# Finer hand-over steps in a sixteen-image, four-layer pipeline on one core

## The chip, the core and the metric

The kernel runs on one core of a Trainium2 chip. The core has a matrix engine (PE, with its weight loads shown as PEld), a vector engine (DVE), a scalar engine (ACT), a general engine (POOL) and a queue engine (SP); sixteen DMA engines move data for SP, ACT and POOL. Each engine works through its own queue in order, and semaphores tie the queues together. The metric is the device time of one execution in microseconds (us). The kernel before took 5924.86 us (median of three runs, 5919.08 to 5937.79).

## The reference

The input is 16 images of 64 x 64 positions (4096 tokens) with 256 channels, all float32. Four layers follow each other, each of the form `x = x + layer(_gn(x))`, where `_gn` is a group norm with 32 groups over a whole image:

```python
# layer 0: nearest of 1024 codes, whose row is added
dis = sum(xf*xf) + sum(e*e, axis=0) - 2*matmul(xf, e);  out = e.T[argmin(dis)]
# layer 1: attention inside each row of 64 positions, sigmoid instead of softmax
attn = sigmoid((x@Wf+bf) @ (x@Wg+bg).T);  out = attn @ (x@Wh+bh)
# layer 2: one scalar gate per token
sm = softmax(x0[:, :, None] * x1[:, None, :], axis=1)
out = sigmoid(einsum('bn,bnm->bm', x2, sm)) * x
# layer 3: linear attention with 4 heads of 32, then a layer norm with scale and shift
q = softmax(q, over head channels)*SCALE;  k = softmax(k, over tokens)
out = layernorm((context(k, v) @ q) @ w_out + b_out) * gamma + beta
```

Because every layer norms over a whole image, no layer can begin on an image before the layer ahead has ended on it.

## The kernel before, in words

One image is cut into 8 chunks (`NCHUNK`) of 512 tokens, each of 4 tiles (`CH`) of 128 tokens. A chunk in channel-major form is a tile of 128 partitions x 2 halves (`k` = 0, 1) x 512 tokens. The work is written as Python generators, one for each stage of one image:

- `stats0` (L287) loads an image's chunks and takes the statistics for the first norm.
- `stage1` (L303) is the search. For each tile T, ACT writes `nn` (L372), PE multiplies the normed chunk `xn` with the codes into `pd` (L377, two banks of PSUM), DVE adds the two and finds the maximum (`nd`, L384), DVE finds its index (L389), and POOL starts a gather that adds the code's row into the token tile `xc` (L390). Once in each chunk there is more: `norm` makes `xn` (L322) and its square `sq` (L325) on ACT, PE sums the squares (`px`, L331), ACT copies the sums (`xrow`, L336) and PE transposes them (`pxt`, L338), from where DVE copies them in `norm_rows` (L343); `back` transposes the four token tiles of the chunk before (`pt`, L352), ACT copies them over the chunk (L355), DVE takes the next norm's statistics (`chunk_stats`, L249), and ACT starts the store (L358).
- `layer1` (L416): `attend` makes `fg` and `h` and the sigmoid `at`; `mix` (L498) multiplies (`po`, L506), adds on DVE (L511), takes statistics and loads the chunk after next.
- `rows2` (L540) makes the three rows of layer 2 for an image: `pr` (L565), `rows` on ACT (L569), three small stores, transposes `prt` (L574) and a DVE copy `x01` (L575).
- `stage2` (L592) is the exponentials: 64 pairs of one ACT exponential of 128 x 2048 (L617) and one DVE product sum (L620).
- `gate2` (L653): each chunk is loaded, `gb` (the gate, broadcast) is loaded, and for each half ACT makes `u` (L674) and DVE applies it (L675); then statistics and a store.
- `stage3` (L689) is layer 3. Its first loop makes `kx` (L746), `qv` (L759 to L764), transposes `kx` (L770, L772), takes the maximum of the queries (`qm`, L778, DVE), subtracts it on POOL (L779), takes the exponential on ACT (L780) and multiplies keys with values (`pc`, L784). `normalize` (L728, POOL) and `queries` (L716, L718) follow one chunk later. The second loop makes the output.

Each `yield n` in a generator says how much work the step before it stood for. A heap at the end of the kernel (L877 on) gives every stage of every image a start and a length, and takes the generators' steps in the order of these times; so several images are always in work, each in another stage, and a step between two yields stays together. The framework's scheduler then orders the instructions of each engine from that order, by priority and by when it takes operands and buffers to be there. The order in a queue is fixed when the kernel is built.

Buffers that matter here: the tag `t4` has 5 slots of 4 KB and is shared by `nn`, `nd`, `sq`, `fg` and `rows`; small PSUM tiles (`bank`) share 4 banks; `pd`, `ph` and layer 1's `po` (`wide`) share 2 slots of two banks; `xa` (search chunks) has 3 slots, `xc` 2, `gb` 1. A wait for a slot is a wait for the last reader of what was in it.

Of the kernel before, what the change touches and what calls it, by code (L numbers as in the profile page):

```python
# [16 lines left out]
P = 128  # L17
# [4 lines left out]
CH = 4  # L22
# [19 lines left out]
def kernel(  # L42
# [244 lines left out]
    def stats0(b):  # L287
# [3 lines left out]
        for ch in range(NCHUNK):  # L291
            xt = xb.tile([P, NK, CW], F32, tag="xb", name=f"xs_{tag}_{ch}")
            nc.sync.dma_start(out=xt, in_=src[:, :, ch * CW : (ch + 1) * CW])
            chunk_stats(st, xt, ch)
            yield 1.5
# [7 lines left out]
    def stage1(b):  # L303
# [4 lines left out]
        xt, xc, xn, nx2, pxt = {}, {}, {}, {}, {}  # L308
# [9 lines left out]
        def norm(ch):  # L318
            xn[ch] = s1p.tile([P, NK, CW], F32, tag="xn", name=f"xn_{tag}_{ch}")
            sq = s1p.tile([P, NK, CW], F32, tag="t4", name=f"sq_{tag}_{ch}", bufs=5)  # L320
            for k in range(NK):
                nc.scalar.activation(  # L322
                    xn[ch][:, k, :], xt[ch][:, k, :], AF.Identity, bias=nbias[:, k : k + 1], scale=scale[:, k : k + 1]
                )
                nc.scalar.activation(  # L325
                    sq[:, k, :], xt[ch][:, k, :], AF.Square, bias=nbias[:, k : k + 1], scale=scale[:, k : k + 1]
                )
            px = bank(f"px_{tag}_{ch}")
            for t in range(CH):
                for k in range(NK):  # L330
                    nc.tensor.matmul(  # L331
                        px[32 * t : 32 * t + 32, :P], lhsT=neg32, rhs=sq[:, k, t * P : (t + 1) * P],
                        start=(k == 0), stop=(k == NK - 1),
                    )
            xrow = small.tile([P, P], F32, tag="xrow", name=f"xrow_{tag}_{ch}", bufs=1)
            nc.scalar.copy(xrow, px[:, :P])  # L336
            pxt[ch] = bank(f"pxt_{tag}_{ch}")
            nc.tensor.transpose(pxt[ch][:, :P], xrow, ident)  # L338

        def norm_rows(ch):  # L340
            px = pxt.pop(ch)
# [6 lines left out]
        def back(ch):  # L348
            for k in range(NK):
                pt = bank(f"pt_{tag}_{ch}_{k}")  # L350
                for t in range(CH):
                    nc.tensor.transpose(  # L352
                        pt[:, t * P : (t + 1) * P], xc[ch][:, t, k * P : (k + 1) * P], ident
                    )
                nc.scalar.copy(xt[ch][:, k, :], pt)  # L355
            chunk_stats(st1, xt[ch], ch)
            d = dram.tile([P, NK, CW], F32, tag=f"x1_{ch}", name=f"x1_{tag}_{ch}")
            nc.scalar.dma_start(out=d, in_=xt.pop(ch))  # L358
            x1_d[b].append(d)
# [3 lines left out]
        norm(0)  # L363
# [3 lines left out]
        for ch in range(NCHUNK):  # L367
            for t in range(CH):
                T = ch * CH + t

# [25 lines left out]
                if t == 1 and ch > 0:  # L396
                    back(ch - 1)
                    yield 2
                if t == 2 and ch + 1 < NCHUNK:
                    norm(ch + 1)  # L400
                    yield 2
                if t == 3:
                    if ch + 1 < NCHUNK:
                        norm_rows(ch + 1)
                        tokens(ch + 1)
                    if ch + 2 < NCHUNK:
                        load(ch + 2)
        back(NCHUNK - 1)
# [7 lines left out]
    def layer1(b):  # L416
# [34 lines left out]
        def attend(ch):  # L451
# [10 lines left out]
            for n in range(2):  # L462
                part = slice(2 * n * CK, 2 * (n + 1) * CK)
                nc.scalar.activation(fg[:, n, :], pfg[part, :HW], AF.Identity, bias=bfg_n[part, :])
            ph = wide(f"ph_{tag}_{ch}").rearrange("p (t c) -> p t c", c=C)
# [12 lines left out]
            yield 5  # L478
# [19 lines left out]
        def mix(ch):  # L498
# [12 lines left out]
            nc.vector.tensor_tensor(X, po.rearrange("p r m i -> p m r i"), X, ALU.add)  # L511
            chunk_stats(st2, xt[ch], ch)
# [10 lines left out]
        for ch in range(NCHUNK):  # L523
# [6 lines left out]
            yield 3  # L530
# [9 lines left out]
    def rows2(b):  # L540
# [17 lines left out]
        for h in range(2):  # L558
# [11 lines left out]
            for n in range(3):  # L570
                nc.scalar.dma_start(out=rd[n, h], in_=rows[n : n + 97 : 32, :])
            pt = bank(f"prt_{tag}_{h}")
# [6 lines left out]
            yield 4  # L579
# [12 lines left out]
    def stage2(b, parts=1):  # L592
# [19 lines left out]
        for part in range(parts):  # L612
# [30 lines left out]
            if rest is not None and part >= parts // 2 - 1:  # L643
                yield next(rest)
# [300 lines left out]
```

## Time and profile before

| | |
|---|---|
| median of the runs | 5924.86 us |
| the profiled execution | 5928.44 us, of which the profile's span is 5926.7 us |
| PE busy | 5337.4 us, 90% of the span |
| DVE busy | 5121.1 us, 86% |
| ACT busy | 4570.8 us, 77% |
| POOL busy | 1939.4 us, 33% |
| mean granted clock of PE | 0.941 |
| moved by DMA | 1059.47 MB, mean 179 GB/s |

How to read it: an engine's busy time is the time in which it executes an instruction. The idle time before an instruction is put down to what released it (the "releaser"). A busy PE is not PE at its peak, since matmuls overlap. With four to six stages in work, idle time on an engine only costs something where that engine or one that waits for it sets the pace.

### The profile page before, as it was taken

The numbers are of one execution on the slowest core, as the hardware profiler recorded it, in microseconds if no ns is written. First come the engines' busy times: TensorE is split into PE (matmuls) and PEld (weight loads), VectorE is DVE, ScalarE is ACT, GpSimd is POOL, SyncE is SP. The second block draws the span as 40 slices with busy tenths as digits, with TensorE's granted clock in tenths as the row PEclk, the third lists the DMA queues.
The fourth block names the chain that finished last, engine by engine and source line by source line (L and its number), as shares of the span: only waits on it lengthen the run. The fifth ranks groups of instructions, "written<-read, shape, count | busy, mean of one in ns | idle before, by whom it ended". The sixth has DMA issues, their size and how long they took to land.

```text
span 5926.7 us, 79561 instructions
## 1 busy us (share of the span) xinstructions
PE 5337.4 (90%) x28239; PEld 3211.1 (54%) x28239; DVE 5121.1 (86%) x7282; ACT 4570.8 (77%) x6754; POOL 1939.4 (33%) x1314
## 2 busy tenths in 40 slices
PE   8968899889999999998989999898999989997777
PEld 3524465545656565564656556565555646564555
DVE  6499798989989898898989889898998989888882
ACT  4377687878778787887879788797878878787873
POOL 3122233224233332433334233342424333231331
PEclk9989999989999898999999899999999999998899
DMA  6544745555656656565665656656565664644543
GB/s 186 162 124 124 225 137 177 184 184 162 207 168 192 197 151 202 184 207 181 184 205 167 194 183 188 206 174 204 164 210 164 202 204 147 209 158 173 184 158 116
DMA packets 521380, 1059.47 MB, mean 179 GB/s; under 512 B 52504, under 2 KB 266392, under 8 KB 512792
## 3 DMA queue, kind: packets, MB, share of 16 engines
q1 hardware_dynamic: 406288, 885.11, 44.7%
q0 software_dynamic: 73728, 67.14, 7.9%
q10 hardware_dynamic: 40968, 102.13, 4.5%
q8 instruction: 224, 3.67, 0.3%
q14 instruction: 172, 1.41, 0.1%
HBM read 751.18 MB, written 303.04 MB: 178 GB/s over the span
## 4 chain that ended last, share of the span: by engine, by line
PE 48%; DVE 16%; ACT 12%; DMA 7%; issue 6%; POOL 4%; ACTq 0%; SPq 0%; POOLq 0%; DVEq 0%
PE pd_s L377 15%; DVE ex_s L620 6%; ACT ex_s L617 5%; PE ph_l L468 5%; PE pqv_s L759 3%; PE po_s L854 3%; PE pk_s L737 3%; PE po_l L506 2%; PE pr_r L565 2%; DMA xr_r<-x_l 2%; DVE i_s L389 2%; POOL qv_s L779 2%; PE pvr_s L834 1%; PE pz_s L826 1%; DMA qo_s<-qd_s 1%
## 5 line engine op out<-in xcount | busy, mean ns | idle before, releaser
L620 DVE CUSTOM_DVE_ANT_0 ex_s<-ex_s,x2b 128x2048 f32<-128x2048 f32 x1024 | 2350.7, 2302 | 46.2 <-ACT ex_s L617 44.9
L617 ACT ACTIVATE ex_s<-x0b,nmax_s,x_r 128x2048 f32<-128x2048 f32 x1024 | 2137.8, 2088 | 66.4 <-DVE num_s L620 60.3
L377 PE MATMUL pd_s<-e,xn_s 128*128 128x512 f32 x4096 | 2022.2, 623 | 43.5 <-DVE m L384 40.8
L390 POOL DMA_INDIRECT xc_s<-in_emb_rows,i_s x512 | 1058.1, 2067 | 2063.9 <-DVE i_s L389 1466.8
L377 PEld LDWEIGHTS pd_s<-e,xn_s 128*128 128x128 f32 x4096 | 754.4, 197 | 764.9 <-issue 669.1
L384 DVE CUSTOM_DVE_ANT_0 nd_s<-pd_s,nn_s 128x1024 f32<-128x1024 f32 x512 | 622.2, 1215 | 174.4 <-ACT nn_s L372 82.1
L389 DVE FIND_INDEX8 i_s<-m,nd_s 128x8 uint32<-128x1024 f32 x512 | 624.1, 1219 | 0.0
L372 ACT ACTIVATE nn_s<-ne,nx_s 128x1024 f32<-128x1024 f32 x512 | 583.2, 1141 | 21.5 <-DVE nx_s L343 15.7
L468 PE MATMUL ph_l<-wh_l,xt_l 128*128 128x256 f32 x2048 | 525.5, 393 | 28.3 <-DVE m L384 16.5
L759 PE MATMUL pqv_s<-wqv_s,xk_s 128*128 128x256 f32 x2048 | 494.6, 382 | 0.0
L759 PEld LDWEIGHTS pqv_s<-wqv_s,xk_s 128*128 128x128 f32 x2048 | 390.9, 192 | 127.5 <-issue 65.5
L468 PEld LDWEIGHTS ph_l<-wh_l,xt_l 128*128 128x128 f32 x2048 | 380.9, 193 | 143.8 <-issue 57.5
L837 POOL TENSOR_TENSOR lrs_s<-lrs_s,mhalf 128x4 f32<-128x4 f32 x128 | 183.0, 1429 | 749.3 <-ACT lrs_s L836 710.5
L857 ACT ACTIVATE y_s<-po_s,lrs_s 128x256 f32<-128x256 f32 x512 | 237.1, 469 | 214.8 <-PE po_s L854 166.2
L854 PE MATMUL po_s<-wctx_s,qo_s 128*128 128x256 f32 x1024 | 336.0, 415 | 32.3 <-ACT y_s L857 31.1
L506 PE MATMUL po_l<-at_l,h_l 64*128 64x64 f32 x4096 | 318.5, 297 | 46.2 <-DVE xt_l L511 42.7
L506 PEld LDWEIGHTS po_l<-at_l,h_l 64*128 64x128 f32 x4096 | 286.5, 206 | 108.5 <-DVE xt_l L511 48.9
L779 POOL TENSOR_TENSOR qv_s<-qv_s,qm_s 128x512 f32<-128x512 f32 x128 | 232.7, 1818 | 312.3 <-DVE qm_s L778 181.7
L728 POOL TENSOR_TENSOR qv_s<-qv_s,qd_s 128x512 f32<-128x512 f32 x128 | 199.8, 1561 | 304.6 <-DVE qd_s L727 252.9
L865 DVE TENSOR_TENSOR y_s<-pxo_s,y_s 128x512 f32<-128x512 f32 x256 | 175.2, 686 | 125.0 <-ACT y_s L857 123.2
L854 PEld LDWEIGHTS po_s<-wctx_s,qo_s 128*128 128x128 f32 x1024 | 178.2, 198 | 172.5 <-ACT y_s L857 84.7
L737 PE MATMUL pk_s<-xk_s,wk_s 128*128 128x512 f32 x512 | 269.6, 650 | 0.0
(195 smaller groups left out, 7519.8 us busy)
## 6 DMA issues: line engine op xcount, KB each, us to landing
xs_s<-in_xT SPq DMA_DIRECT2D x128, 512.0 KB
xt_s<-in_xT SPq DMA_DIRECT2D x128, 512.0 KB
xc_s<-in_x SPq DMA_DIRECT2D x128, 512.0 KB
x_s<-xt_s ACTq DMA_DIRECT2D x128, 512.0 KB
xt_l<-x_s SPq DMA_DIRECT2D x128, 512.0 KB
x_l<-xt_l SPq DMA_DIRECT2D x128, 512.0 KB
xr_r<-x_l SPq DMA_DIRECT2D x128, 512.0 KB
xg_g<-x_l SPq DMA_DIRECT2D x128, 512.0 KB
```

What stands on the lines that cost most here:

```text
L372: nc.scalar.activation(nn, ne2, AF.Identity, bias=nx2[ch][:, t : t + 1])
L377: nc.tensor.matmul(pd[:, cols], lhsT=xn[ch][:, k, t * P : (t + 1) * P], rhs=e2[:, k, cols], start=(k == 0), stop=(k == NK - 1),)
L384: nc.vector.tensor_tensor_reduce(out=nd, in0=pd, in1=nn, scale=1.0, scalar=-3.0e38, op0=ALU.add, op1=ALU.max, accum_out=m8[:, 0:1],)
L389: nc.vector.max_index(i8, m8, nd)
L390: nc.gpsimd.indirect_dma_start(out=xc[ch][:, t, :], out_offset=None, in_=emb_rows, in_offset=bass.IndirectOffsetOnAxis(ap=i8[:, 0:1], axis=0),
L468: nc.tensor.matmul(ph[:, t, :], lhsT=X[:, k, t * P : (t + 1) * P], rhs=wh_n[:, k, :], start=(t % 2 == 0 and k == 0), stop=False, skip_grou ...
L506: nc.tensor.matmul(po[:, r, k * CH + t, :], lhsT=h[rows, t, k * P : (k + 1) * P], rhs=at[rows, t, :], start=True, stop=True,)
L617: nc.scalar.activation(ex, x0b, AF.Exp, bias=nmax[:, T : T + 1], scale=x01[:, T, 1:2], accum_out=den[:, h, T : T + 1])
L620: nc.vector.tensor_tensor_reduce(out=ex, in0=ex, in1=x2b, scale=1.0, scalar=0.0, op0=ALU.mult, op1=ALU.add, accum_out=num[:, h, T : T + 1],)
L737: nc.tensor.matmul(pk, lhsT=wk_n[:, k, :], rhs=xt[:, k, :], start=(k == 0), stop=(k == NK - 1))
L759: nc.tensor.matmul(pqv[:, j, :], lhsT=xt[:, k, t * P : (t + 1) * P], rhs=wqv_n[:, k, :], start=(j == 0 and k == 0), stop=False, skip_group ...
L854: nc.tensor.matmul(po[:, j, :], lhsT=qT[:, t * P : (t + 1) * P], rhs=wctx[:, 1, :], start=True, stop=True)
```

## The change

No arithmetic is changed. Every engine issues the same number of instructions as before (17117 on PE, 6772 on DVE, 6005 on ACT, 1351 on POOL and 1827 on SP in the built programs, before PE's instructions are split in two); what changes is where steps end, in which step an instruction lies, and a few buffers.

- `stats0` and `gate2` yield after each half of a chunk. In `gate2` the second half's `u` is written over `gb`, which gets 2 slots; `u` gets 1.
- In `stage1`, `norm` is done in halves, after tiles 1 and 2 of the chunk before; the sums of the squares (`norm_sums`) come ahead of tile 3; the transposition of the sums moves to `norm_rows` after tile 3. `back` does two tiles at a time, both halves in one bank, after tiles 0 and 1; its statistics come after tile 2. `load` of the chunk after next comes ahead of tile 3, and `tokens` after tile 2, both one tile earlier than before.
- `layer1` yields between `fg` and `ph`, and between `mix` and its statistics and load. `rows2` yields ahead of its transposes. `stage2` of the last image takes twice as many steps of `gate2`, which are half as long.
- `stage3` yields between `kx` and `qv`, between the two halves of `qv`, and after the maximum; `queries` comes after the subtraction, and the exponential after `pc`.

```diff
@@ stats0
-            chunk_stats(st, xt, ch)
-            yield 1.5
+            for k in range(NK):
+                nc.vector.bn_stats(st[:, k, ch, :], xt[:, k, :])
+                yield 0.75
@@ stage1
-        def norm(ch):
-            for k in range(NK):
+        def norm(ch, k):
+            if k == 0:
...
+            for out_, func in ((xn[ch], AF.Identity), (sq[ch], AF.Square)):
                 nc.scalar.activation(
...
+        def norm_sums(ch):
...
-            pxt[ch] = bank(f"pxt_{tag}_{ch}")
-            nc.tensor.transpose(pxt[ch][:, :P], xrow, ident)
...
         def norm_rows(ch):
-            px = pxt.pop(ch)
+            px = bank(f"pxt_{tag}_{ch}")
+            nc.tensor.transpose(px[:, :P], xrow.pop(ch), ident)
...
-        def back(ch):
+        def back(ch, pr):
+            pt = bank(f"pt_{tag}_{ch}_{pr}").rearrange("p (k n) -> p k n", k=NK)
             for k in range(NK):
-                pt = bank(f"pt_{tag}_{ch}_{k}")
-                for t in range(CH):
+                for j in range(2):
                     nc.tensor.transpose(
-                        pt[:, t * P : (t + 1) * P], xc[ch][:, t, k * P : (k + 1) * P], ident
+                        pt[:, k, j * P : (j + 1) * P], xc[ch][:, 2 * pr + j, k * P : (k + 1) * P], ident
                     )
-                nc.scalar.copy(xt[ch][:, k, :], pt)
-            chunk_stats(st1, xt[ch], ch)
+            nc.scalar.copy(xt[ch][:, :, 2 * pr * P : 2 * (pr + 1) * P], pt)
+            if pr == 1:
...
+                if t == 3:
+                    if ch + 2 < NCHUNK:
+                        load(ch + 2)
+                    if more:
+                        norm_sums(ch + 1)
+                        yield 0.7
...
                 yield 4
-                if t == 1 and ch > 0:
-                    back(ch - 1)
-                    yield 2
-                if t == 2 and ch + 1 < NCHUNK:
-                    norm(ch + 1)
-                    yield 2
-                if t == 3:
-                    if ch + 1 < NCHUNK:
-                        norm_rows(ch + 1)
+                if t < 2 and ch > 0:
+                    back(ch - 1, t)
+                    yield 0.7
+                if t in (1, 2) and more:
+                    norm(ch + 1, t - 1)
+                    yield 0.7
+                if t == 2:
+                    if more:
                         tokens(ch + 1)
-                    if ch + 2 < NCHUNK:
-                        load(ch + 2)
+                    if ch > 0:
+                        chunk_stats(st1, xt.pop(ch - 1), ch - 1)
+                        yield 0.7
+                if t == 3 and more:
+                    norm_rows(ch + 1)
@@ layer1
+            yield 1.5
             ph = wide(f"ph_{tag}_{ch}").rearrange("p (t c) -> p t c", c=C)
...
-            yield 5
+            yield 3.5
...
+
+        def after(ch):
             chunk_stats(st2, xt[ch], ch)
             if ch + 2 < NCHUNK:
                 load(ch + 2)
...
             mix(ch)
-            yield 3
+            yield 1.5
+            after(ch)
+            yield 1.5
@@ rows2
+            yield 2
             pt = bank(f"prt_{tag}_{h}")
...
-            yield 4
+            yield 2
@@ gate2
-            gb = s3p.tile([P, CW], F32, tag="gb", name=f"gb_{tag}_{ch}", bufs=1)
+            gb = s3p.tile([P, CW], F32, tag="gb", name=f"gb_{tag}_{ch}", bufs=2)
...
-                u = s3p.tile([P, CW], F32, tag="u2", name=f"u_{tag}_{ch}_{k}")
+                u = s3p.tile([P, CW], F32, tag="u2", name=f"u_{tag}_{ch}_{k}", bufs=1) if k == 0 else gb
...
-            chunk_stats(st3, xt, ch)
-            yield 4
+                nc.vector.bn_stats(st3[:, k, ch, :], xt[:, k, :])
+                yield 2
@@ stage3
+            yield 1.5
             qv = s3p.tile([P, CH, 2, P], F32, tag="u4", name=f"qv_{tag}_{ch}")
...
+                if pr == 0:
+                    yield 1
...
-            yield 5
+            yield 2.5
...
-            if ch > 0:
-                queries(ch - 1)
...
             nc.gpsimd.tensor_tensor(q4, q4, qm.unsqueeze(3).to_broadcast([P, CH, HEADS, DH]), ALU.subtract)
-            nc.scalar.activation(qv[:, :, 0, :], qv[:, :, 0, :], AF.Exp)
+            yield 2
+            if ch > 0:
+                queries(ch - 1)
+                yield 1
...
-            yield 5
+            nc.scalar.activation(qv[:, :, 0, :], qv[:, :, 0, :], AF.Exp)
+            yield 2
```

## The prediction

> **What bounds the kernel now.** I read the page's busy times first, then the windows by stage, then the waits of each engine in the stretch where the pipeline is full, then the queue of SP. The busy shares and the chain that ended last:
>
> ```profile
> PE 5337.4 (90%) x28239; PEld 3211.1 (54%) x28239; DVE 5121.1 (86%) x7282; ACT 4570.8 (77%) x6754; POOL 1939.4 (33%) x1314
> ...
> PE 48%; DVE 16%; ACT 12%; DMA 7%; issue 6%; POOL 4%; ACTq 0%; SPq 0%; POOLq 0%; DVEq 0%
> ```
>
> No engine is full and none is far from it: PE holds the chain for half the time, and the rest is hand-over between engines. The windows (columns: stretch, its length, busy time and instructions of PE, PEld, DVE, ACT, POOL, then PE's granted clock, DMA share, GB/s) show the regimes:
>
> ```profile
> 320.00:360.00 40.00, 27.21 (x90) 11.61 (x89) 40.00 (x53) 34.52 (x38) 11.28 (x5) 0.87 0.48 145
> ...
> 2368.00:2664.00 296.00, 282.58 (x1563) 173.43 (x1560) 270.76 (x389) 248.62 (x365) 108.37 (x69) 0.99 0.63 194
> 2664.00:2960.00 296.00, 274.14 (x1473) 165.06 (x1474) 269.57 (x389) 246.35 (x366) 114.01 (x75) 0.97 0.59 182
> ```
>
> At the start DVE is full. From 592 to 5328 us (sixteen such windows, 4736 us) PE is busy 4399 us by the sum of the rows and DVE 4252, so PE is idle 337 us there and DVE 484. That idle time is all this change can win, for it leaves every busy time alone. The waits of that stretch that the edits touch (engine, what waits, for whom: us, times, longest):
>
> ```profile
> PE px_s L331 <- ACT sq_s L325: 52.5, 47, 3.7
> ...
> PE pt_s L352 <- DMA xc_s<-in_emb_rows,i_s: 17.0, 7, 4.1
> ...
> PE pt_s L352 <- ACT kx_s L746: 12.3, 7, 2.0
> ...
> PE pxt_s L338 <- ACT xrow_s L336: 10.8, 19, 1.3
> ...
> DVE x_r L575 <- PE prt_r L574: 94.6, 27, 8.5
> ...
> DVE st_s L249 <- ACT xt_s L355: 13.8, 20, 2.5
> ...
> ACT qv_s L780 <- POOL qv_s L779: 122.9, 82, 3.6
> ...
> ACT xrow_s L336 <- PE px_s L331: 49.2, 40, 3.0
> ```
>
> They have one form: an engine comes to an instruction whose input went round over another engine, and too little other work stands between. Against this stands SP's own queue over the whole run, where the loads wait for buffers:
>
> ```profile
> SPq L312 <- DMA x_s<-xt_s: 528.6, 98, 8.5
> SPq L667 <- ACT u_g L674: 433.3, 86, 14.1
> ...
> SPq L316 <- DMA xc_s<-in_emb_rows,i_s: 265.6, 36, 27.1
> ...
> SPq L316 <- PE pt_s L352: 211.7, 85, 7.5
> ```
>
> **The change part by part.** Where I say how much work stands between two instructions, it is counted in the built order of both kernels, images 2 to 13, each instruction at its row's duration. Gains are negative; brackets hold both ends.
>
> *Norm in halves.* PE's wait of 52.5 us for the squares goes nearly whole, since the sums now stand a tile after the first half: -45 on PE [-52.5, 0]. PE's work between the sums and their transposition grows from a median of 0.9 us to 4.1: -10 [-10.8, 0]. ACT's copy of the sums still follows in the same step; the work ahead of it grows only from 2.3 to 4.0 us: -20 of 49.2 on ACT [-49.2, 0]. Against it: a square now stays in one of the five `t4` slots about a tile (296/32 = 9 us) longer. In eleven images 7 of 352 `nn` take the slot of the `nn` of the tile just before, where none did; each waits for a DVE addition (1.22 us) and a hand-over, with exponentials queued behind it on ACT and `nd` on DVE waiting: +10 on ACT for 512 tiles [0, +25].
>
> *Tokens two tiles at a time.* The first pair's gathers are long done, the second pair waits as before: -8 of PE's 17.0 [-17, 0]. (Another 39 us of this wait lie between 200 and 592 us, where DVE is full and covers them; were DVE not full, they would be worth up to 20.) One bank instead of two at a time, and none held for the transposed sums through tile 3: -6 of 12.3 [-12.3, 0]. Statistics a tile later than the copy: -12 of 13.8 on DVE [-13.8, 0]. On SP, `load` and `tokens` (128 DMAs each) go one tile earlier, past whatever SP issues in that tile; priced below as a rival, 0 here.
>
> *Rows.* On DVE the copy `x01` stood (image 6), for the second half, after product 29, while `rows` on ACT stood after exponential 30; now the copy stands after product 31 and the next layer's maximum, `rows` after exponential 31. So one exponential (2.09 us) less is waited for, 14 times: -29. In the first half an `nd` whose `nn` stands behind `rows` now comes ahead of the copy, and part of the wait passes to it: half as much, -14. Together -43 of 94.6 on DVE [-94.6, 0]; PE's own wait for `rows` (10.1): -6 [-10.1, 0].
>
> *Gate.* `u` on ACT waits for `gb` 12.0 us and DVE for `u` 9.0: -8 and -7 [each to 0]. SP's 433.3 us behind one `gb` slot go with the second slot; the loads queued behind come sooner, and the largest wait on such a load, PE's for `xr`, is 46.9 us in the stretch: 0 taken [-47, +47, if the new order collides instead]. Writing `u` over `gb` adds no wait to ACT, which read it last; the `gb` load two chunks on waits for DVE instead.
>
> *Layer 3.* Between the last copy of `qv` and its exponential ACT's other work grows from a median of 5.3 us to 8.1 (lowest tenth 2.3 to 4.2); the way round is a DVE maximum of 0.68, POOL's 1.82 and two hand-overs. Half of 122.9: -60 on ACT [-123, 0]. PE's `pc` after `ek`: -2. A new wait: in chunk 0 of eleven images the work between the exponential and the copy `qT` falls from 6.3 to 2.8 us, less than the reduction, reciprocal, POOL product and transposes between them (0.68 + 0.24 + 1.56 + 0.43): +20 on ACT [0, +39] and +5 on PE [0, +39], with the exponentials queued behind.
>
> *Layer 1, statistics, last image.* `psc` waits 8.5 us in all: -3 on PE [-8.5, 0]. Splitting a 1.36 us pair of statistics costs nothing, same instructions. The last image's steps come in the same order: 0 [-10, +10].
>
> Sum: PE -45 -10 -8 -6 -6 -2 -3 +5 = -75; DVE -12 -43 -7 = -62; ACT -20 +10 -8 -60 +20 = -58. Weighted with the chain's shares (0.48, 0.16, 0.12) that is -36 -10 -7 = -53. Were PE the only bound, it would be -75. I take the middle, -64, because PE is nearest to full in the stretch but the chain leaves it for half the time. The profiled execution took 5928.4 us, so 5864; it lay 3.6 us above the median, so 5861 against the runs.
>
> Every removed PE wait is also clock: the window with PE busy 282.58 us was granted 0.99, its neighbour with 274.14 us 0.97, the stretch at 320 us with 27.21 of 40 only 0.87. If 75 us less idle raised the mean by 0.02, 4399 us of PE would shrink by some 88. I take 0, because two neighbouring windows do not separate cause from mix, and keep -88 as an end. [...]
>
> [...]
>
> **The rivals.** *The time comes back as slot waits (5915).* PE also waits for DVE to free PSUM (`po` 42.7, `pd` 21.6, `ph` 14.1 and 11.8, 90 us together). If DVE sets the pace, PE's removed waits reappear there, and only DVE's -62 at its chain share remains, -10. For it: DVE is full at the start. Against: DVE has 484 us idle in the stretch. That the edits do nothing because the scheduler orders by itself is ruled out: the distances above are in the built order.
>
> *SP's queue stands longer (5988, slower).* The search's loads move a tile nearer to the release of their slots, and SP stands still in front of them; everything behind it, layer 2's `xr` and layer 3's `qo` first, comes late. These two cost PE 46.9 + 16.8 = 63.7 us in the stretch now. If they triple, +127 - 64 = +63. It decides once they more than double. For it: these loads wait 1006 us on SP already. Against: `gb` gives back up to 433 us.
>
> *The clock follows (5773).* The sum and the end of -88 together.
>
> **How the numbers follow.** The forecast has 0.55 (own range 5815 to 5905), slot waits 0.14, SP's queue 0.19, the clock 0.12. No change is within 0.3% (5907 to 5943), about what a measurement of this kernel can tell. Faster: 0.55 + 0.12 + half of the slot waits = 0.74; same: the other half and a little of SP's = 0.08; slower 0.18. The range goes from 5775, just above the clock's case, to 5975, short of SP's tripled waits, with about a tenth left on each side.
>
> **What would show it.** Right: `px` waiting for squares under 10 us, `x01` for `prt` under 45, the query exponential for POOL under 70, PE idle in the full stretch near 270 us. Wrong: `xr` and `qo` above 130 us together, `nn` waiting for `m` by tens of us, `po` and `pd` waiting for DVE by 90 us more, or `qT` and `pq` behind POOL by more than 40.

## Result and the profile after

The changed kernel takes 5976.9 us (median of four runs, 5974.92 to 5981.46) against 5930.62 us for the kernel before on the same chip (four runs, 5919.08 to 5937.79). The ratio is 1.0081, with a 95% interval from 1.0061 to 1.0101: 46 us slower, where 64 us faster was forecast. The profiled execution took 5974.92 us, 2 us under the median, with a span of 5973.2 us.

The busy times and the chain that ended last, from the page of the kernel after:

```profile
PE 5361.9 (90%) x28239; PEld 3231.7 (54%) x28239; DVE 5154.9 (86%) x7282; ACT 4576.8 (77%) x6754; POOL 1914.7 (32%) x1314
...
PE 53%; ACT 9%; DVE 7%; issue 4%; DMA 3%; POOL 3%; SPq 0%; POOLq 0%; ACTq 0%; DVEq 0%
```

The same instructions keep PE 24.5 us longer (5337.4 before) and DVE 33.8 us longer (5121.1 before).

Now the waits that the prediction showed or named, with the largest new ones of ACT, in the same stretch (592 to 5328 us) of the kernel after. The columns are engine, what waits, for whom: us in all, times, longest:

```profile
ACT d_n L262 <- PE pg_n L260: 75.3, 49, 2.8
...
DVE nd_s L396 <- ACT nn_s L384: 74.8, 59, 4.8
...
ACT qT_s L739 <- PE pq_s L737: 63.6, 25, 6.8
...
DVE x_r L597 <- PE prt_r L596: 40.4, 16, 9.9
...
ACT qv_s L816 <- POOL qv_s L801: 34.0, 17, 2.6
...
ACT xn_s L324 <- DMA xt_s<-in_xT: 33.0, 14, 6.7
...
ACT xrow_s L339 <- PE px_s L334: 20.5, 43, 1.0
...
DVE st_s L249 <- ACT xt_s L358: 0.7, 2, 0.4
```

And PE's own, of the same stretch and kernel:

```profile
PE pd_s L389 <- DVE m L396: 99.7, 43, 4.3
PE pq_s L737 <- POOL qv_s L749: 79.6, 23, 5.4
PE pg_n L259 <- DVE mv_n L256: 37.5, 14, 2.8
PE pt_s L355 <- DMA xc_s<-in_emb_rows,i_s: 29.7, 16, 7.3
...
PE po_l L523 <- DVE xt_l L528: 19.2, 12, 3.6
...
PE pr_r L586 <- DMA xr_r<-x_l: 9.2, 15, 2.0
...
PE pz_s L852 <- DMA qo_s<-qd_s: 2.5, 3, 1.5
...
PE pxt_s L343 <- ACT xrow_s L339: 1.3, 1, 1.3
...
PE px_s L334 <- ACT sq_s L324: 0.7, 1, 0.7
```

Almost every wait that the edits aimed at fell. PE's wait for the squares fell from 52.5 to 0.7 us, ACT's for POOL from 122.9 to 34.0, DVE's for the transposed rows from 94.6 to 40.4. But PE found others: `pd` waiting for DVE rose from 21.6 to 99.7, `pq` waiting for POOL from 3.1 to 79.6, the norm's `pg` from 12.9 to 37.5. So PE's idle time in this stretch did not fall to 270 us: by the window it is 4736 - 4368.1 = 368 us, against 337 before.

Since the work of an image is the same in each, a fair stretch has the same work in both kernels. I take ten images, from the first multiplication of `wo` (`pw`) in one image to that ten images later. Windows (stretch, length, busy time and instructions of PE, PEld, DVE, ACT, POOL, then PE's clock, DMA share, GB/s), before:

```profile
1483.80:5005.60 3521.80, 3288.48 (x17640) 1994.01 (x17640) 3168.98 (x4506) 2846.34 (x4208) 1244.66 (x810) 0.95 0.60 187
```

and after, with the head and the tail:

```profile
0.00:1486.40 1486.40, 1287.39 (x6629) 710.35 (x6630) 1223.59 (x1763) 1052.44 (x1468) 468.95 (x300) 0.93 0.54 165
1486.40:5041.20 3554.80, 3308.85 (x17641) 2013.92 (x17640) 3213.07 (x4509) 2850.40 (x4211) 1190.95 (x811) 0.94 0.59 186
5041.20:5973.20 932.00, 765.66 (x3972) 507.47 (x3970) 718.28 (x1012) 673.96 (x1077) 254.79 (x205) 0.89 0.50 165
```

Of the 46.5 us between the spans, 3 lie in the head, 33 in the ten images (352.2 us each before, 355.5 after) and 11 in the tail. Of the 33, PE is busy 20.4 us longer at a granted clock of 0.94 in place of 0.95, and idle 12.6 us longer. So the larger part of the loss in these ten images is not idle time of PE but a longer busy time for the same instructions.

### The profile page after: what moved, and what is told of

Its sections match the earlier page's. It is cut to its first block, busy times and chain, and to the rows that moved or that the text cites. A ratio compares the mean times of both kernels' runs of the same rounds, so it can differ in the third digit from the quotient of the medians.

```text
span 5973.2 us, 79609 instructions
## 1 busy us (share of the span) xinstructions
PE 5361.9 (90%) x28239; PEld 3231.7 (54%) x28239; DVE 5154.9 (86%) x7282; ACT 4576.8 (77%) x6754; POOL 1914.7 (32%) x1314
## 4 chain that ended last, share of the span: by engine, by line
PE 53%; ACT 9%; DVE 7%; issue 4%; DMA 3%; POOL 3%; SPq 0%; POOLq 0%; ACTq 0%; DVEq 0%
PE pd_s L389 18%; PE pqv_s L781 5%; ACT ex_s L639 5%; PE ph_l L485 4%; PE po_s L880 3%; PE pk_s L758 3%; DVE ex_s L642 3%; PE po_l L523 2%; PE pc_s L809 2%; PE pr_r L586 2%; PE pfg_l L473 2%; PE pz_s L852 1%; PE pvr_s L860 1%; PE pxo_s L885 1%; DMA xt_s<-in_xT 1%
## 5 line engine op out<-in xcount | busy, mean ns | idle before, releaser
L642 DVE CUSTOM_DVE_ANT_0 ex_s<-ex_s,x2b 128x2048 f32<-128x2048 f32 x1024 | 2396.6, 2346 | 74.5 <-ACT ex_s L639 73.8
L389 PE MATMUL pd_s<-e,xn_s 128*128 128x512 f32 x4096 | 2066.5, 635 | 155.8 <-DVE m L396 124.9
L402 POOL DMA_INDIRECT xc_s<-in_emb_rows,i_s x512 | 1117.9, 2183 | 2035.9 <-DVE i_s L401 1451.5
L384 ACT ACTIVATE nn_s<-ne,nx_s 128x1024 f32<-128x1024 f32 x512 | 585.1, 1144 | 13.0 <-DVE nx_s L345 10.8
L485 PE MATMUL ph_l<-wh_l,xt_l 128*128 128x256 f32 x2048 | 497.7, 381 | 1.6 <-DVE xt_l L528 1.1
L863 POOL TENSOR_TENSOR lrs_s<-lrs_s,mhalf 128x4 f32<-128x4 f32 x128 | 160.5, 1254 | 842.9 <-ACT lrs_s L862 825.4
L749 POOL TENSOR_TENSOR qv_s<-qv_s,qd_s 128x512 f32<-128x512 f32 x128 | 247.5, 1933 | 221.8 <-DVE nkm_s L764 98.2
L523 PEld LDWEIGHTS po_l<-at_l,h_l 64*128 64x128 f32 x4096 | 259.7, 191 | 99.7 <-issue 49.0
L523 PE MATMUL po_l<-at_l,h_l 64*128 64x64 f32 x4096 | 290.2, 281 | 21.5 <-DVE xt_l L528 19.2
L801 POOL TENSOR_TENSOR qv_s<-qv_s,qm_s 128x512 f32<-128x512 f32 x128 | 202.9, 1585 | 252.0 <-DVE qm_s L800 150.6
L324 ACT ACTIVATE xn_s<-xt_s,nb_n,s_n 128x512 f32<-128x512 f32 x256 | 202.0, 807 | 87.6 <-DMA xt_s<-in_xT 70.3
```

The costliest lines, as they stand in the source:

```text
L384: nc.scalar.activation(nn, ne2, AF.Identity, bias=nx2[ch][:, t : t + 1])
L389: nc.tensor.matmul(pd[:, cols], lhsT=xn[ch][:, k, t * P : (t + 1) * P], rhs=e2[:, k, cols], start=(k == 0), stop=(k == NK - 1),)
L402: nc.gpsimd.indirect_dma_start(out=xc[ch][:, t, :], out_offset=None, in_=emb_rows, in_offset=bass.IndirectOffsetOnAxis(ap=i8[:, 0:1], axis=0),
L485: nc.tensor.matmul(ph[:, t, :], lhsT=X[:, k, t * P : (t + 1) * P], rhs=wh_n[:, k, :], start=(t % 2 == 0 and k == 0), stop=False, skip_grou ...
L523: nc.tensor.matmul(po[:, r, k * CH + t, :], lhsT=h[rows, t, k * P : (k + 1) * P], rhs=at[rows, t, :], start=True, stop=True,)
L642: nc.vector.tensor_tensor_reduce(out=ex, in0=ex, in1=x2b, scale=1.0, scalar=0.0, op0=ALU.mult, op1=ALU.add, accum_out=num[:, h, T : T + 1],)
```

## The experiments

The theories, with the letters that the expectations use:

- A: one new collision makes the loss. On POOL the normalisation of one chunk's queries now stands behind the subtraction of the next chunk, so `pq` comes late, and its lateness goes round.
- B: slot waits. DVE frees the PSUM slots of `pd` too late, and any wait of PE that goes comes back there.
- C: the search's new order costs by itself.
- N: within the search, the norm in pieces has a price of its own.
- P: POOL and DVE slow each other when they meet; the change makes them meet more often.
- K: the tokens two at a time, or their later statistics, have a price of their own.
- L: the price is that of the pairs' layout in a bank.
- S: no part has a price of its own. The order of every queue is built once from one list of due times, so an edit anywhere re-deals what meets what, and a meeting that costs is repeated in every image.

In the tables below, "us per image" and "idle" (PE's idle time per image) are from ten full images, measured as above, in the one profiled execution of each kernel; that execution lay up to 17 us from the median in the second column. The medians come from several sets of runs, each with the kernel before in it, so kernels of different sets are compared by their distance from the kernel before.

### The inverted pair on POOL

What theory A looks like in the kernel after, in the timeline around 2416 us (start, us, engine, line, operation, what it writes and reads, form; in brackets the idle time before it and its releaser):

```profile
2416.43 5.09 DVE L642 CUSTOM_DVE_ANT_0 ex_s<-ex_s,x2b 128x2048 f32<-128x2048 f32 x1
...
2416.71 1.65 POOL L801 TENSOR_TENSOR qv_s<-qv_s,qm_s 128x512 f32<-128x512 f32 x1
2417.72 1.64 POOL L749 TENSOR_TENSOR qv_s<-qv_s,qd_s 128x512 f32<-128x512 f32 x1
...
2419.42 1.12 PE L737 MATMUL pq_s<-ident,qv_s 128*128 128x128 f32 x4 [4.87 <-POOL qv_s L749]
```

PE stands 4.87 us for `pq`, and its releaser, the normalisation (L749), stands behind the subtraction (L801). The kernel before never has them in this order. The experiment puts them back in the old order in the kernel after (the code is shortened):

```diff
-            nc.gpsimd.tensor_tensor(q4, q4, qm..., ALU.subtract)
+            with tc.issue_after(done.ins) if done is not None else ExitStack():
+                nc.gpsimd.tensor_tensor(q4, q4, qm..., ALU.subtract)
```

> The changed kernel, with one edge of order added on POOL: the subtraction of a chunk of queries is queued behind the normalisation of the chunk before. In the changed kernel the two stand the other way round for chunks 1 and 0 of eleven images. Theory A (the inverted pair on POOL is the cause): PE's wait of pq for POOL falls from 89.7 us to under 20, the product sums of 5.09 us, one in each of those images, go (the mean of the product sum falls from 2346 ns to about 2305), and the time falls from 5977 to between 5915 and 5945. Theory B (slot waits: DVE frees the pd slots too late, and any PE wait that goes comes back there): pq's wait goes too, but pd's wait for DVE grows beyond 125 us, and the time stays within 5960 to 5985. Theory C (the search's new order costs by itself): 5960 to 5985 as well, with pd's wait near 125 us.

Measured: 5950.15 us, ratio 1.0036 [1.0022, 1.0051], 26 us nearer to the kernel before than the kernel after is. But the wait is still there, as PE's waits of this kernel show:

```profile
PE pd_s L389 <- DVE m L396: 97.1, 43, 4.1
PE pq_s L737 <- POOL qv_s L749: 68.8, 23, 4.0
```

With the two POOL instructions in the old order in every image, 69 of the 80 us remain, so their order is not what makes `pq` late, and `pd` waits as before. Nor does the wait need the inverted pair: in the kernel before with the other edits (below) the pair is never inverted, and `pq` waits 53.8 us for POOL. Theory A's chain is not confirmed, although the edit gave back 26 us; the time lies between the ranges of A and of B and C, and nearly neutral shifts (below) bring as much.

### Whole stages undone or done alone

Layer 3 as before in the kernel after; layer 3 alone on the kernel before; the search as before in the kernel after; and everything except search and layer 3 on the kernel before. The edits are the hunks of the change, stage by stage.

> The changed kernel with layer 3 (stage3) as before. Theory A: the inverted pair is gone, so 5900 to 5945, at or under the kernel before if the other parts bring what was forecast of them. Theory B: 5950 to 5985, the pd wait for DVE stays above 100 us. Theory C: 5950 to 5985.

> The kernel before with layer 3 (stage3) alone changed. In its built order the inverted pair stands in one image only, at chunk 1. Theory A: so no loss, 5900 to 5935; the exponential's wait for POOL falls from 144.8 us to under 70. Theory B: within 15 us of before, 5915 to 5945, and pd waits more for DVE. If layer 3's new steps cost by something else than the pair, 5950 or more.

> The changed kernel with the search (stage1) as before. The inverted pair is gone in its built order too. Theory A: 5900 to 5945. Theory C (the search's new order costs): 5900 to 5930, and the pd wait for DVE falls back to about 41 us. Theory B: 5960 to 5985, with px waiting for the squares again (64 us) in place of pd waiting for DVE.

> The kernel before with everything else changed: layer 1, rows, statistics, exponentials of the last image and gate, but the search and layer 3 as before. The changed kernel with the old search took 5900 and the kernel before with layer 3 alone 5955. If parts add up, these parts alone are worth 5900 - 5955 = -55, so 5875. If they don't (each edit shifts the whole order), 5895 to 5930.

| kernel | us | ratio to before [95%] | us per image | idle |
|---|---|---|---|---|
| kernel after | 5976.9 | 1.0081 [1.0061, 1.0101] | 355.5 | 24.6 |
| after, layer 3 as before | 5998.5 | 1.0124 [1.0100, 1.0148] | 358.5 | 28.6 |
| before with the new layer 3 | 5954.6 | 1.0045 [1.0028, 1.0061] | 354.4 | 25.8 |
| after, search as before | 5900.2 | 0.9952 [0.9935, 0.9970] | 347.3 | 20.5 |
| before with the other edits | 5987.5 | 1.0091 [1.0072, 1.0109] | 354.7 | 26.6 |

Two of the four lie outside every range that was expected for them: layer 3 as before (5998.5, at most 5985 expected) and the other edits (5987.5, at most 5930). The old search falls where A and C had put it, the new layer 3 where "something else than the pair" was to cost.

The parts do not add. The new layer 3 alone costs 24 us and the other edits alone 56; both together, with the old search, do not cost 80 but gain 30. Layer 3 costs 24 us on the kernel before and saves 22 in the kernel after. The kernel with the old search, 5900.2 us, beats both kernels. PE's waits in it, 592 to 5328 us:

```profile
PE px_s L332 <- ACT sq_s L326: 52.3, 38, 2.0
...
PE pd_s L378 <- DVE m L385: 25.9, 23, 4.6
```

It keeps the wait of 52 us that the change was to remove, and in this stretch `pq` does not wait for POOL at all: that wait, which lies in layer 3, went with an edit of the search. This is one order, though: no shift was tried on this kernel, so how much of its 30 us is the luck of that order is open.

### Inside the search

The norm as before in the kernel after (tokens new), and the tokens as before in the kernel after (norm new):

> The changed kernel with the norm in stage1 as before (one piece after tile 2, sums and transposition in it); the rest of stage1, tokens two tiles at a time and earlier loads among it, stays changed. The search as before in the changed kernel gave 5900, so some part of the search's change costs 77 us. Theory N (the norm in pieces): 5890 to 5920, pd waits for DVE under 60 us. Theory K (tokens in pairs, statistics later): 5955 to 5985. Theory S (the schedule as a whole shifts at each edit, no part carries the cost): somewhere between, 5920 to 5955.

> The changed kernel with the tokens going back four tiles at a time and their statistics at once, as before; the norm in pieces and the earlier loads stay. Theory N: 5955 to 5985. Theory K: 5890 to 5920. Theory S: 5920 to 5955.

Measured: 5969.9 us (1.0079 [1.0058, 1.0101]) and 5937.7 us (1.0020 [1.0006, 1.0034]), so 44 and 12 us above the kernel before, where the kernel after lies 46 above. The norm in pieces makes a difference of 2 us; the tokens in pairs with later statistics make one of 35. The first lies in K's range; the second is less of a gain than K expected and lies in the range of S.

These two runs also tell where PE's largest new wait comes from. With the norm as before it is

```profile
PE pd_s L383 <- DVE m L390: 37.5, 32, 4.9
```

and with the tokens as before

```profile
PE pd_s L388 <- DVE m L395: 64.7, 28, 4.8
```

against 99.7 us in the kernel after, 25.9 with the whole search as before, and 115.1 with the new search but the old layer 3. So this wait does follow the search's edits, the norm in pieces most of all. But it does not set the time: with the norm as before 62 us of it go, and the kernel gains 2.

So I took the tokens alone to the kernel before:

```diff
-                if t == 1 and ch > 0:
-                    back(ch - 1)                       # four tiles, then statistics
-                    yield 2
+                if t < 2 and ch > 0:
+                    back(ch - 1, t)                    # two tiles, both halves in one bank
+                    yield 0.7
...
+                if t == 2 and ch > 0:
+                    chunk_stats(st1, xt.pop(ch - 1), ch - 1)
+                    yield 0.7
```

> The kernel before with one part alone: the tokens go back two tiles at a time, with their statistics after tile 2. Theory K: slower by 20 to 45 us, 5945 to 5975. Theory P: slower only if the product sums' excess grows above 2 us an image; otherwise 5915 to 5945.

Measured: 6031.7 us, 1.0155 [1.0134, 1.0176], 100 us slower, where K expected 20 to 45. (The mean of the product sums rose from 2302 to 2335 ns, so this run alone speaks for P too.) So this edit looked like the culprit, and I took it apart: pairs without new steps (both in the old step, statistics at once), pairs in two steps with statistics at once, and late statistics alone.

> The kernel before with the token tiles transposed two at a time into one bank for both halves, but both pairs and the statistics in one step after tile 1, as the four were. Before takes 5930 us, pairs with two steps and late statistics took 6032. Theory K (what costs is that the transposes and copies are spread over two steps, or the late statistics): 5915 to 5945, because here neither is. Theory L (what costs is the bank layout: a copy needs both halves of its pair): 6000 to 6040. Theory S (the order of every queue is fixed from one priority list, and any edit re-deals it; no part has a price of its own): anything between 5900 and 6030, not predictable from the parts.

> The kernel before with pairs in two steps after tiles 0 and 1, but the statistics in the same step as the second pair. Theory K, if the two steps cost: 6000 to 6040; if the late statistics cost: 5915 to 5945. Theory L: 6000 to 6040. Theory S: anything between 5900 and 6030, and the distances of this run, of the one with pairs together and of the one with late statistics alone from the kernel before do not add up to the 102 us of all three.

> The kernel before with the four token tiles as before, but the statistics after tile 2 instead of at once after the copies. Theory K, if the late statistics cost: 6000 to 6040; if the two steps cost: 5915 to 5945. Theory L: 5915 to 5945. Theory S: anything between 5900 and 6030.

| kernel before, with | us | ratio to before [95%] | us per image | idle |
|---|---|---|---|---|
| nothing | 5928.8 | 1 | 352.2 | 23.3 |
| pairs, one step | 5918.6 | 0.9984 [0.9969, 0.9999] | 350.5 | 22.9 |
| pairs, two steps, statistics at once | 6135.7 | 1.0343 [1.0321, 1.0364] | 369.8 | 34.4 |
| late statistics alone | 6169.0 | 1.0408 [1.0389, 1.0427] | 370.7 | 38.5 |
| pairs, two steps, late statistics | 6031.7 | 1.0155 [1.0134, 1.0176] | 359.2 | 29.5 |

The layout costs nothing here (theory L falls). The two steps (with the layout) and the late statistics cost over 200 us each, and both together 100. No price per edit that adds up gives that. But both also lie beyond 6030, the end that S had given.

A rival to S is not separated in this table. A step's `yield` moves all later steps of its stage, and these edits change the sum of the search's yields, which in the kernel before is 160 up to the end of its last chunk, just the total that the heap is told for one period. Late statistics add 0.7 in each of seven chunks, so the search's last steps are due 4.9/160 of a period later, some 11 us at 352 us; two steps with statistics at once take 4.2 away, some 9 us earlier; both together add only 0.7. The two costliest kernels are the two whose search is out of step, in opposite directions, and the two departures cancel where both edits are made. That this is what costs over 200 us is argued from the code; no run changes the yields alone.

A large part of where the 240 us of late statistics go can be seen in PE's waits of that kernel, 592 to 5328 us:

```profile
PE pq_s L719 <- POOL qv_s L731: 84.3, 11, 7.8
PE pd_s L376 <- DVE m L383: 69.6, 45, 3.9
PE pw_s L805 <- DVE ctxbd_s L802: 45.8, 10, 4.6
PE pbr_r L554 <- ACT wrow_n L549: 44.9, 11, 5.2
```

Read the counts: 11, 10, 11. These are waits of 4 to 8 us that come once in nearly each image of the stretch, and they lie in layer 3 and layer 2, far from the statistics that were moved. The three make 175 us (27.4 in the kernel before); `pd`, in the search, waits 48 us more. In the kernel with pairs in two steps and statistics at once, others take their place:

```profile
PE pr_r L570 <- DMA xr_r<-x_l: 72.5, 24, 4.5
PE po_l L511 <- DVE m L385: 60.9, 14, 5.2
PE pq_s L721 <- POOL qv_s L733: 46.7, 11, 4.6
PE pbr_r L556 <- ACT wrow_n L551: 34.7, 11, 3.2
```

### Nearly neutral shifts

If the order decides, then an edit that moves no step of the search should move the time as well. `LAGR` sets when layer 2's rows start after layer 1, in periods of an image; `LAG2` when the exponentials start after the rows.

```diff
-LAGR = 0.03
+LAGR = 0.035
```

on the kernel before, on the kernel after, and on the kernel before with the tokens in pairs and late statistics:

> The kernel before with one number changed that belongs to no step of the change: the rows stage of each image begins 0.005 image later (about 1.8 us of a period of 352 us). No instruction is added, removed or resized; only the built order moves a little. Theories N and K, in which a part has its own price: within 10 us of before, 5920 to 5940. Theory S (the order as a whole decides): it may move by as much as single parts did, more than 15 us either way.

> The same shift of 0.005 image in the changed kernel. Theories N and K: within 10 us of the changed kernel, 5967 to 5987. Theory S: more than 15 us from it, either way.

> The kernel with pairs alone (6032 us) with one neutral edit: layer 2's rows start 0.035 instead of 0.03 of a period after layer 1. The same edit moved the kernel before by +2 to +6 us and the changed kernel by -20 us. Theories K and L (pairs have a price of their own): 6010 to 6050. Theory S (the 102 us are one deal of the order): nearer to the kernel before, 5930 to 6000.

Measured: 5932.0 us (1.0013 [0.9996, 1.0029]), 5956.9 (1.0057 [1.0034, 1.0079]) and 5971.9 (1.0075 [1.0059, 1.0092]). The first hardly changes, against S and as N and K expected; the second's distance from the kernel before falls from 46 to 31 us and the third's from 100 to 43, as S expected. Then a second shift, on late statistics alone and on the kernel before:

```diff
-LAG2 = 0.17
+LAG2 = 0.175
```

> The kernel with late statistics alone (6169 us, +240 over the kernel before) with layer 2's exponentials started 0.175 instead of 0.17 of a period after the rows, which is some 2 us at 352 us a period, and re-deals the order of every queue. Late statistics with a price of their own: 6140 to 6200, and 200 to 280 us above the kernel before with the same new lag. Theory S (the 240 us are this deal of the order): 100 us or more away from 6169, and the difference from the kernel before with the same lag is under 120 us.

> The kernel before with the same new lag, 0.175 instead of 0.17. If the order of before is one deal among many (theory S), this lies anywhere between 5900 and 6170, more likely above 5930 than below, since the four other small edits of the search gave -10, +102, +207 and +240. If a later start of 2 us is all that it is, 5925 to 5945.

Measured: 6040.7 us (1.0186 [1.0159, 1.0214]) and 5953.8 us (1.0041 [1.0027, 1.0055]). Starting the exponentials some 2 us later moves late statistics by -127 us and the kernel before by +26 (distances from the kernel before in the same runs). Both lie where S put them. The cost of the same edit, with the same yields, is 240 us under one lag and 87 under the other. It was positive both times, so a part of it may be a price of its own (K); two lags can't say how much.

### POOL against DVE

The 5.09 us product sum in the timeline above is twice as long as its usual 2.28, and two POOL instructions lie beside it. Theory P makes this the loss. The test leaves the subtraction of the maximum on POOL out (the softmax of the queries is then taken without it) in both kernels:

```diff
-            nc.gpsimd.tensor_tensor(q4, q4, qm..., ALU.subtract)
```

> The changed kernel without POOL's subtraction of the maximum from the queries (128 pieces of 128 x 512; the maximum is still taken on DVE, the exponential is taken of the queries as they are). Theory P (POOL and DVE shut each other out: over the ten full images a product sum that meets a POOL piece on the way takes up to 5.09 us instead of 2.28, 5.4 us of DVE in each image, against 0.4 in the kernel before): the excess falls below 2 us an image and the time falls by 40 us or more, to 5937 or less, and by at least 25 us more than the same edit brings to the kernel before. Theory K (tokens in pairs put the transposes and their copies in the way, whatever POOL does): the time falls only as far as in the kernel before.

> The kernel before without the same subtraction. Its product sums lose only 0.4 us an image to POOL, but its exponential waits 144.8 us for POOL. Theory P: little to win from POOL itself, 5905 to 5930. Theory K says nothing else here; if ACT's wait for POOL is what costs, the gain is larger, 5880 or less.

Measured: the kernel after without it 5975.3 us (1.0067 [1.0049, 1.0086]), the kernel before without it 5917.7 us (0.9975 [0.9956, 0.9993]). The product sums (group by line: busy us, mean ns | idle before, releaser) of the kernel after

```profile
L642 DVE CUSTOM_DVE_ANT_0 ex_s<-ex_s,x2b 128x2048 f32<-128x2048 f32 x1024 | 2396.6, 2346 | 74.5 <-ACT ex_s L639 73.8
```

and of the same kernel without the subtraction

```profile
L642 DVE CUSTOM_DVE_ANT_0 ex_s<-ex_s,x2b 128x2048 f32<-128x2048 f32 x1024 | 2340.3, 2290 | 97.9 <-ACT ex_s L639 96.8
```

DVE's instructions became 56 us shorter in sum, and the time some 2 us. The meeting is real, but DVE waits 23 us longer for the exponentials instead. Theory P had expected 40 us or more, and 25 more than in the kernel before, which gained 14; so it falls as the cause of the loss. That the meetings cost nothing is not shown, since an instruction left out shifts the order too.

## Why the prediction was wrong

The forecast was wrong in sign, and the range (5775 to 5975) missed the median by 2 us. By its own steps, in the stretch of its waits:

| step | forecast (us) | measured (us) |
|---|---|---|
| norm: `px` for squares, PE | -45 | 52.5 to 0.7: -52 |
| norm: `pxt`, PE | -10 | 10.8 to 1.3: -10 |
| norm: `xrow`, ACT | -20 | 49.2 to 20.5: -29 |
| `t4` slots, ACT | +10 | `nn` for `m` 2.7 to none: -3 |
| tokens: gathers, PE | -8 | 17.0 to 29.7: +13 |
| tokens: statistics, DVE | -12 | 13.8 to 0.7: -13 |
| rows: `x01`, DVE | -43 | 94.6 to 40.4: -54 |
| gate: `u` for `gb`, ACT | -8 | 12.0 to 6.6: -5 |
| gate: DVE for `u` | -7 | 9.0 to 2.8: -6 |
| layer 3: exponential for POOL, ACT | -60 | 122.9 to 34.0: -89 |
| layer 3: `qT`, ACT | +20 [0, 39] | 7.7 to 63.6: +56 |
| layer 3: `pq`, PE | +5 [0, 39] | 3.1 to 79.6: +77 |
| `xr` and `qo`, PE | 0 [-47, 47] for `xr` | 63.7 to 11.7: -52 |
| `pd` for DVE, PE | only in the slot rival | 21.6 to 99.7: +78 |
| norms: `pg` for DVE, PE | not named | 12.9 to 37.5: +25 |
| `xn` for its load, ACT | 0, but for the SP rival | 4.2 to 33.0: +29 |
| busy times, whole span | 0 | PE +24.5, DVE +33.8 |

*The removed waits were right.* Each was followed through the built order, and each but the gathers and the gate's two came out about as forecast or went further. Its four signs of being right show it: `px` under 10, `x01` under 45, the exponential under 70, all three so; only the fourth, PE idle near 270 us, failed (368), and it was the one that counted. Of the signs of being wrong, `qT` and `pq` behind POOL came true (their sum rose by 132 us, where 40 was the mark).

*The step that failed is the sum.* It set the removed waits of three engines against only the new waits that had been looked for (-75 on PE, with +5 for `pq` as PE's only new wait), and so took the rest of the schedule as unchanged, every busy time with it. On PE alone the two largest new waits, `pd` and `pq`, are +155, more than the -75 and the further -52 of `xr` and `qo` together. And PE's busy time grew by 24.5 us over the span, more than half of the 46.5 us between the spans. The experiments show why adding part by part could not find this: of the two, only `pd` follows the edits of its own part, and a wait that an edit takes away does not come off the time. The wait of `pq`, in layer 3, is 0 in the same stretch in the kernel with the new layer 3 and the old search, and 84 in the kernel where nothing but the search's statistics moved.

*The mis-sized term.* `pq` was bounded by 39 us, from the distances in chunk 0. It measured 77 more. The bound set the work in between against the chain's instructions at their own durations; that each of them must first get its turn on ACT, DVE and POOL was left out. (That this makes up the difference is argued, not shown.) Putting the two POOL instructions back in order took only 11 us off it.

*The clock.* The prediction took 0 and kept -88 as an end; PE's busy time rose by 20 us in the ten images instead, clock 0.95 to 0.94. In the trace of the kernel before, the clock was granted at half from 0.7 us after a wait of PE of 2.63 us (for the squares, one of the waits that the change removes) and from 1.1 us after one of 2.02 us (for layer 1's `psc`, ended at 921.33 us), with no longer wait in the 6.9 us ahead (first the end of the first wait, then the two stretches):

```profile
614.52 0.41 PE L331 MATMUL px_s<-sq_s,neg 128*32 128x128 f32 x2 [2.63 <-ACT sq_s L325]
```

```profile
615.20:622.00 6.80, 6.80 (x36) 3.99 (x35) 4.93 (x8) 3.21 (x6) 1.55 (x1) 0.50 0.83 278
...
922.40:929.20 6.80, 6.80 (x36) 5.62 (x34) 6.80 (x9) 3.95 (x9) 4.12 (x4) 0.50 0.63 198
```

That these two waits brought the half clock on is not shown; with nearly all of the waits for the squares gone (52.5 to 0.7 us), the mean clock of the kernel after is 0.932, below the 0.941 of the kernel before. Nor does PE's idle time as a whole decide. The shifted kernel after has

```profile
PE 5386.3 (90%) x28239; PEld 3240.0 (54%) x28239; DVE 5131.2 (86%) x7282; ACT 4581.4 (77%) x6754; POOL 1922.8 (32%) x1314
```

in a span of 5958.3 us, so PE is idle 572 us, less than the 589 of the kernel before, and yet the span is 32 us longer: PE is busy 49 us longer, at a mean clock of 0.931 against 0.941. What sets the clock here stays open.

*The rivals.* "SP's queue stands longer" was to give the slower result, through `xr` and `qo`; together they fell to a fifth, so the sign came by another way. SP's waits after, over the whole run:

```profile
SPq L537 <- DVE xt_l L528: 541.3, 93, 23.9
...
SPq L317 <- DMA xc_s<-in_emb_rows,i_s: 319.7, 45, 20.4
...
SPq L313 <- DMA x_s<-xt_s: 211.5, 41, 8.5
```

The wait behind the one `gb` slot (433.3 us) is gone, `load` waits less for its slots' stores (528.6 before; a wait for the later statistics, 184.4 in place of 54.7, takes back part), `tokens` and layer 1's store wait more (265.6 and 277.4). PE's waits for `xr` and `qo` do not show it, but ACT does: its `xn` waits 33.0 us for the search's load, 4.2 before. What that costs PE is not shown. "Slot waits" named PE's waits for DVE to free PSUM; of its 90 us more, `pd` brought 78, while `po` fell by 23.5 and the loss went past its 5915. It was the nearest of the rivals, but not the whole. The `t4` slots, for which the prediction took +10 on ACT, show no wait of `nn` for a slot in the stretch after (2.7 us before). (The prediction's tile of 9 us took a window of 296 us for an image; with 352 us an image it is 11.)

*What is shown and what stays open.* Shown: the loss is not a sum of prices of parts. Layer 3 costs 24 us on one kernel and saves 22 on another, the other edits cost 56 alone, undoing the search gains 76, the same edit costs 240 or 87 us under two lags 2 us apart, and part of the waits that pay for it lies in other stages. Not shown: which of PE's new waits starts the others in the kernel after, and why PE's busy time grew. The one edit that aimed at `pq` took it only from 79.6 to 68.8, and the norm as before took 62 us off `pd` without much gain. Nor is it settled whether late statistics have a price of their own under 87 us, or whether it is their weight in the list of due times that costs.

## What to carry to other kernels

In a pipeline whose queues are ordered once at build time, with two engines over 85% busy, the waits that an edit removes were no forecast here: compare them with the spread that nearly neutral shifts of the order give (here 6 and 26 us on the kernel before, and 15 to 127 us on edited ones) before a gain of their size is believed. A wait whose count is near the number of images is likely one meeting repeated in each; look for these first, in every stage and not only in the edited one. Try a set of edits in subsets: here the best kernel, 30 us faster than before, was the change without its largest part. And when parts are taken singly, keep the sum of a stage's yields the same, or the part is not all that changes.

## What the runs showed of the hardware

- The DVE product sums (two inputs of 128x2048) of the kernel after took 2.28 us at the median; the one at 2416.43 us took 5.09, with two POOL tensor operations of 128x512 recorded beside it (1.65 and 1.64 us). The product is 2.81 us longer there, and the two POOL operations cover 2.65 us together. Not every meeting lengthened the product: the one at 2409.98 us took 2.29, with a subtraction of 1.78 us recorded on POOL from 2411.39 on. Without the subtraction the mean of the product sums falls from 2346 to 2290 ns in the kernel after, while the time falls by some 2 us. What makes the product of 5.09 us long can't be read from this timeline, where it is recorded 0.28 us ahead of the subtraction (starts on POOL are rough).
- PE's busy time for the same 28239 matmuls was not constant: 5303.3 us with the tokens as before, 5325.3 with the old search, 5337.4 before, 5361.9 after, 5386.3 after with the shift and 5425.3 with pairs in two steps and statistics at once, at mean granted clocks of 0.937, 0.947, 0.941, 0.932, 0.931 and 0.927. PE's idle time does not order them: it is 635 us in the first of these and 572 in the fifth. Nor does the mean clock alone, since the first has the least busy time at a lower clock than the next two.
- In the kernel before, PE's clock was granted at half (0.50 for 6.8 us) after waits of 2.02 and 2.63 us, with no longer wait in the 6.9 us ahead of either (the rows under "The clock").
